# Block fetches spread over slots, deeper buffers and reordered last steps in a one-core attention and mixture-of-experts layer

## Chip, cores and metric

The kernel runs on one core of one Trainium2 chip. The metric is the device time of one execution in microseconds, on the slowest (here the only) core; lower is better. Several runs are taken, and their median is the kernel's time.

## What is computed

The input x has shape (8, 256, 256): eight sequences of 256 tokens, 2048 tokens in all, with 256 features, in float32. Two residual sub-layers follow each other:

```python
x = x + layernorm(attention(layernorm(x)))
x = x + layernorm(experts(layernorm(x)))
```

Attention has 16 query heads and 4 key/value heads of size 128, layer norms on queries and keys, rotary tables and a causal softmax. The second sub-layer, which the change concerns, sends each token to two of eight experts and adds a shared one:

```python
weights, indices = top_k(softmax(xf @ gate_w.T), 2)      # per token, renormalised
h = silu(xf @ w_gate[e]) * (xf @ w_up[e])                # 176 hidden units, e chosen
out = sum over the two e of weight_e * (h @ w_down[e])
out += sigmoid(xf @ shgate_w) * ((silu(xf @ shw_gate) * (xf @ shw_up)) @ shw_down)
```

## The kernel before

**Attention** comes first, sequence by sequence, as a pipeline of small steps written out in a fixed order (lines 325 to 789). For each tile of 128 tokens it ends in the normalised rows, which are written to a table `xf_rows` in DRAM (L606), and in the routing: which two experts, with which weights, at which place of that expert's list (L617 to L702).

**The experts' stage** starts at L1043. All tokens' choices are sorted by expert into NB = 39 blocks of 128 rows, every block for one expert. The tokens are cut into four groups (ENDS = 4, 9, 13, 16 tiles), and the blocks are laid out group after group, so that after block FULL[g] (15, 25, 33, 39) all results for the tiles of group g are there. `table`, `rows_of` and `sources` work out which token stands in which row of which block (`src`); `experts` (L881) works out the addresses `offs` of each block's weights, which TensorE's sequencer loads into registers four blocks at a time (L959).

A loop over slots s = 0 to NB + 2 (L1064) is a software pipeline in a hand-written order. Each engine has one queue and goes through it in this order; it waits only where an instruction needs a semaphore. In slot s stand:

- `fetch` of later blocks (L939): an indirect DMA, issued on GpSimd (POOL), gathers 128 rows from `xf_rows` into a buffer `xb`. There are AHEAD + 1 = 13 buffers; a fetch whose buffer is still to be read waits for that block's transposes on TensorE.
- `turn_block(s)` (L947): two transposes on TensorE into `xt`, a copy `xT` on VectorE.
- `open_block(s - 1)` (L956): four weight-load and matmul passes into `gu`; ScalarE takes the silu into `slb` (L973), VectorE multiplies into `h` (L975).
- `close_block(s - 3)` (L988): matmuls into `py`, a copy `yb` on ScalarE (L998, three buffers), and a DMA of the block's 128 result rows to a table `ys` in DRAM, issued on SP (L999).
- `turn_hidden(s - 2)` (L979): transposes of `h` and a copy on ScalarE (L985).
- one step of the shared expert (`fill(1)`, L1080), while any are left; `fill(n)` takes the next n steps of the list that L297 makes. A step has matmuls (L270 or L286), an activation on ScalarE and, for L270, a product on VectorE (L279). It has nothing on POOL or SP.
- for tiles whose time has come (`when`, L1055 to L1060): `collect` (L1002), two indirect DMAs on POOL that gather a tile's two result rows per token from `ys`; two slots later `combine` (L1013), four VectorE steps, and after each odd tile a power on POOL (L1033) that gives both tiles' reciprocal deviations; then `leave_tile` (L1037), two VectorE steps (L251, L1040) and a DMA of the finished tile on SP (L1041).

The tiles of the last group are collected behind the loop (L1090), which also finishes the shared expert.

The fetches are paced in the program's order by this line; with four fetched ahead of the loop, it lets two stand in each slot until the fetches are 12 blocks ahead, then one:

```python
for b in range(ready, min(ready + 2, s + AHEAD + 1, NB)):
    fetch(b)
    ready = b + 1
```

Of the kernel before, what the change touches and what calls it, by code (L numbers as in the profile page):

```python
# [9 lines left out]
F32 = mybir.dt.float32  # L10
# [9 lines left out]
P = 128  # L20
B, S, HID = 8, 256, 256
# [14 lines left out]
NB = T * TOPK // P + E - 1  # L36
# [6 lines left out]
FULL = [end * TOPK + E - 1 for end in ENDS]  # L43
# [4 lines left out]
def block_kernel(  # L48
# [89 lines left out]
    for j, w in enumerate((wg, wu)):  # L138
# [22 lines left out]
        fill=NEG,  # L161
# [87 lines left out]
    def norm_apply(dst, src, name):  # L249
        mean, rstd = stats.pop(name)  # L250
        nc.vector.tensor_scalar(dst, src, mean, rstd, ALU.subtract, ALU.mult)  # L251
# [67 lines left out]
    def fill(n):  # L319
        for f in todo[:n]:  # L320
            f()
        del todo[:n]


    with ExitStack() as actx:
# [406 lines left out]
        with tc.manual_schedule():  # L732
# [7 lines left out]
            for s in range(B * NS + OUT + 5):  # L740
# [4 lines left out]
                u, j = s - LAG, s  # L745
# [56 lines left out]
    fw = ctx.enter_context(tc.tile_pool(name="fw", bufs=3))  # L802
# [31 lines left out]
    def table():  # L834

        pn = ps_tr.tile([P, NP], F32, tag="tr", name="total")
        nc.tensor.matmul(
            pn, lhsT=ones, rhs=count.rearrange("p g e -> p (g e)"), start=True, stop=True
        )
        n = fc.tile([P, NP], U32, name="n")  # L840
        nc.vector.tensor_scalar(n, pn, P - 1.0, None, ALU.add)
        nc.vector.tensor_scalar(n, n, P.bit_length() - 1, None, ALU.logical_shift_right)
        upto = nb[:, E:]
        nc.vector.tensor_copy(upto, n)

        end = fc.tile([P, NP], F32, name="end")
        nc.vector.tensor_tensor_scan(
            end, upto, nb[:, :NP], 0.0, ALU.add, ALU.subtract
        )

        off = fc.tile([P, NP], F32, name="off")
        nc.vector.tensor_sub(off, upto, end)
        nc.vector.tensor_add(off, off, lift.rearrange("p g e -> p (g e)"))
        nc.vector.tensor_sub(jump[:, : NP - 1], off[:, 1:], off[:, : NP - 1])

        past = fc.tile([P, NP], F32, name="past")
        more = fc.tile([P, 1], F32, name="more")
        nc.vector.scalar_tensor_tensor(
            past, end, part, jump, ALU.is_le, ALU.mult, accum_out=more
        )  # L860
        pickT = fc.tile([P, P], F32, name="pickT")
        nc.vector.tensor_scalar(pickT, aside, more, None, ALU.is_equal)
        load["pickT"], load["upto"], load["off"] = pickT, upto, off

    def rows_of():
        ps = ps_tr.tile([P, NB], F32, tag="tr", name="pickp")
        nc.tensor.transpose(ps, load["pickT"][:NB, :], ident[:NB, :NB])
        pick = fc.tile([P, NB], F32, name="pick")
        nc.vector.tensor_copy(pick, ps)
        load["pick"] = pick  # L870

    def sources():
        ps = ps_tr.tile([P, NB], F32, tag="tr", name="whose")
        nc.tensor.matmul(ps, lhsT=member, rhs=load["pick"], start=True, stop=True)
        src = fc.tile([P, NB], U32, name="src")
        nc.vector.tensor_copy(src, ps)
        load["src"] = src
        load["row"] = ps_tr.tile([1, NB], F32, tag="tr", name="row")
        nc.tensor.matmul(load["row"], lhsT=part, rhs=load["pick"], start=True, stop=True)

    def experts():  # L881

        er = fc.tile([1, NB], I32, name="er")
        nc.vector.tensor_copy(er, load["row"])
        nc.vector.tensor_scalar(er, er, (T // P).bit_length() - 1, None, ALU.logical_shift_right)
        eb = fc.tile([1, NB], F32, name="eb")
        nc.vector.tensor_copy(eb, er)
        nc.vector.tensor_scalar_min(eb, eb, E - 1.0)
        offs = fc.tile([1, 2, NB + LB], I32, name="offs")
        nc.vector.memset(offs, 0)  # L890
        for k, w in enumerate((2 * HE, HID)):
            nc.vector.tensor_scalar_mul(offs[:, k, :NB], eb, float(w))
        load["offs"] = offs
# [40 lines left out]


    state = {}
    AHEAD = 12

    def fetch(b):  # L939
        x_b = fw.tile([P, HID], F32, tag="xb", name=f"xb_{b}", bufs=AHEAD + 1)  # L940
        nc.gpsimd.indirect_dma_start(  # L941
            out=x_b, out_offset=None, in_=xf_rows,
            in_offset=bass.IndirectOffsetOnAxis(ap=load["src"][:, b : b + 1], axis=0),
        )
        state["x", b] = x_b

    def turn_block(b):  # L947
        tr = ps_tr.tile([P, KC, P], F32, tag="tr", name=f"xt_{b}")
        x_b = state.pop(("x", b))
        for c in range(KC):  # L950
            nc.tensor.transpose(tr[:, c, :], x_b[:, c * P : (c + 1) * P], ident)  # L951
        xT = fw.tile([P, KC, P], F32, tag="xT", name=f"xT_{b}")
        nc.vector.tensor_copy(xT, tr)
        state["xT", b] = xT
# [24 lines left out]
    def turn_hidden(b):  # L979
        tr = ps_tr.tile([P, KC, P], F32, tag="tr", name=f"ht_{b}")  # L980
        h = state.pop(("h", b))
        for c in range(KC):
            nc.tensor.transpose(tr[:, c, :], h[:, c * P : (c + 1) * P], ident)  # L983
        hT = fw.tile([P, KC, P], F32, tag="hTb", name=f"hTb_{b}")
        nc.scalar.copy(hT, tr)  # L985
        state["hT", b] = hT

    def close_block(b):  # L988
        hT = state.pop(("hT", b))
        py = ps_sc.tile([P, HID], F32, tag="sc", name=f"py_{b}")  # L990
        off = state.pop(("doff", b))
        for c in range(KC):
            nc.tensor.matmul(  # L993
                py, lhsT=hT[:, c, :], rhs=wd_sb[:, c, bass.ds(off, HID)],
                start=(c == 0), stop=(c == KC - 1),
            )
        y = fw.tile([P, HID], F32, tag="yb", name=f"yb_{b}")
        nc.scalar.copy(y, py)  # L998
        nc.sync.dma_start(out=ys[b * P : (b + 1) * P, :], in_=y)  # L999

# [36 lines left out]
    def leave_tile(i):  # L1037
        y = state.pop(("yo", i))
        norm_apply(y, y, f"d_{i}")
        nc.vector.tensor_add(y, y, x_all[:, i, :])  # L1040
        nc.sync.dma_start(out=out[i * P : (i + 1) * P, :], in_=y)  # L1041

    with tc.manual_schedule():  # L1043
        table()
        fill(2)
        rows_of()
        fill(2)
        sources()
        fill(4)
        ready = 4  # L1050
        for b in range(ready):
            fetch(b)
        experts()

        when = {}  # L1055
        for g, end in enumerate(ENDS):
            begin = ENDS[g - 1] if g else 0
            step = (FULL[g + 1] - FULL[g]) / (end - begin) if g + 1 < G else 0.0
            for i in range(begin, end):
                when[i] = FULL[g] + 3 + int((i - begin) * step)  # L1060
        finding = places()
        late = ENDS[-2]
        LATE = 5
        for s in range(NB + 3):  # L1064
            for b in range(ready, min(ready + 2, s + AHEAD + 1, NB)):
                fetch(b)
                ready = b + 1
            if s < NB:
                turn_block(s)
            if 0 <= s - 1 < NB:  # L1070
                open_block(s - 1)
            if 0 <= s - 3:
                close_block(s - 3)
            if 0 <= s - 2 < NB:
                turn_hidden(s - 2)
            if 2 <= s < G + 3:
                next(finding)

            if s >= 8 and len(todo) > LATE:
                fill(1)  # L1080
            for i in range(late):
                if when[i] == s:
                    collect(i)
            for i in range(late):
                if when[i] == s - 2:
                    combine(i)
                if i % 2 == 1 and when[i] == s - 3:
                    leave_tile(i - 1)
                    leave_tile(i)
        for i in range(late, NTILES):  # L1090
            collect(i)
        fill(LATE)
        for i in range(NTILES):
            if when[i] > NB:
                combine(i)
            if i % 2 == 1 and when[i] > NB - 1:
                leave_tile(i - 1)
                leave_tile(i)
        assert not todo


# [45 lines left out]
```

## Time and profile before

| what | us |
|---|---|
| median of 3 runs | 849.34 |
| lowest and highest run | 846.38, 850.0 |
| the profiled execution | 845.26 |
| its span, first to last instruction | 843.6 |
| mean granted TensorE clock of it | 0.973 of full speed |
| experts' stage: first fetch to the last instruction | 671.1 to 843.6 |

| instructions of the stage | count | mean us of one |
|---|---|---|
| fetch, POOL, L941 | 39 | 0.97 |
| collect, POOL, L1007 | 32 | 0.98 |
| write of block results, SP, L999 | 39 | 128 KB each |
| write of a finished tile, SP, L1041 | 16 | 128 KB each |

The span is what the profile covers, from the first instruction to the last; the profiled execution's own time has 1.66 us more around it. The page gives busy times by engine (PE is TensorE's matmuls, PEld its weight loads, DVE VectorE, ACT ScalarE, POOL GpSimd, SP SyncE); a timeline gives each instruction's start and duration and, in brackets, how long the engine had been idle before it and what ended that. "issue" and "remote" there mean that nothing in the profile, or a signal whose sender it doesn't tell, ended it. Matmuls' ends are modelled, not observed.

### The profile page before, as it was taken

To read this page: it belongs to the slowest core of one execution; us is meant where nothing else is said; L and a number is where in the kernel's file an instruction comes from. 1 tells how busy PE (TensorE), PEld (TensorE's weight loads), DVE (VectorE), ACT (ScalarE), POOL (GpSimd) and SP (SyncE) were. 2 spreads that over 40 slices of the span, in tenths; PEclk is the share of its full clock that TensorE was granted. 3 is DMA by queue.
4 is the path that set the end of the run, shared out by engine and by line. 5 is a ranking of instruction groups with operands and counts; after the bars stand their busy time and mean duration, and the time that the engine had idled before them with its cause. 6 is when DMAs were issued, how large, how long until landed. Compare 5 with 4: busy or idle time off the path is not lost. (4 is left out here: it accounts for less than half of the span.)

```text
span 843.6 us, 11873 instructions
## 1 busy us (share of the span) xinstructions
PE 751.6 (89%) x3770; PEld 552.9 (66%) x3770; DVE 552.8 (66%) x1392; ACT 433.5 (51%) x1393; POOL 486.2 (58%) x523
## 2 busy tenths in 40 slices
PE   4478999999999999999999999998979949998891
PEld 1245667777676677777767777776858827776661
DVE  4586666788778778877877886677644423225675
ACT  1247767656657666675766567565512313333330
POOL 3387587667848757684875768386111162244543
PEclk9789999999999999999999999999999988999997
DMA  8500000000000000000000000004002032224442
GB/s 264 161 1 1 1 1 1 7 1 7 7 1 7 1 7 1 7 7 2 7 1 7 2 7 7 1 7 138 7 13 75 13 94 82 63 88 112 139 126 75
DMA packets 27485, 32.66 MB, mean 39 GB/s; under 512 B 3040, under 2 KB 23616, under 8 KB 27424
## 3 DMA queue, kind: packets, MB, share of 16 engines
q1 hardware_dynamic: 24016, 22.59, 8.5%
q0 software_dynamic: 3408, 9.31, 4.0%
q8 instruction: 31, 0.51, 0.2%
q14 instruction: 30, 0.25, 0.1%
HBM read 22.59 MB, written 9.31 MB: 38 GB/s over the span
## 5 line engine op out<-in xcount | busy, mean ns | idle before, releaser
L366 PE MATMUL qkv<-w_qkv,xnT 128*128 128x512 f32 x384 | 186.6, 610 | 7.3 <-DVE w_qkv L231 3.2
L408 ACT ACTIVATE qn<-qkv,rstds 128x128 f32<-128x128 f32 x320 | 91.2, 368 | 160.7 <-POOL rstds L399 160.7
L399 POOL TENSOR_TENSOR rstds<-ves,nhalf 128x4 f32<-128x4 f32 x80 | 86.9, 1086 | 115.4 <-DVE ves L390 115.4
L434 POOL TENSOR_TENSOR t<-qn,sg_q 128x256 f32<-128x256 f32 x128 | 121.9, 971 | 50.5 <-ACT qn L408 50.5
L581 PE MATMUL o<-wo_sb,oT 128*128 128x256 f32 x512 | 127.2, 387 | 0.0
L482 PE MATMUL sc<-kT,q 128*128 128x128 f32 x768 | 110.1, 278 | 0.9 <-ACT q L471 0.9
L513 ACT ACTIVATE ex<-sc,nmx 128x128 f32<-128x128 f32 (+1 forms) x256 | 107.6, 453 | 2.7 <-DVE nmx L502 2.4
L562 PE MATMUL av<-pT,v 128*128 128x256 f32 (+1 forms) x320 | 101.1, 430 | 7.9 <-ACT oT L573 7.2
L366 PEld LDWEIGHTS qkv<-w_qkv,xnT 128*128 128x128 f32 x384 | 68.1, 197 | 59.9 <-issue 50.4
L482 PEld LDWEIGHTS sc<-kT,q 128*128 128x128 f32 x768 | 102.1, 194 | 4.4 <-ACT q L471 2.4
L581 PEld LDWEIGHTS o<-wo_sb,oT 128*128 128x128 f32 x512 | 91.9, 192 | 9.4
L455 DVE TENSOR_TENSOR t<-t,t 128x512 f32<-128x512 f32 x80 | 55.3, 691 | 51.3 <-POOL t L447 51.3
L470 PEld LDWEIGHTS tq<-ident,t 128*128 128x128 f32 x320 | 38.6, 142 | 69.3 <-issue 50.3
L447 POOL TENSOR_TENSOR t<-t,bb_q 128x512 f32<-128x512 f32 x64 | 81.6, 1275 | 3.0
L549 DVE COPY pT<-tp 128x512 f32<-128x512 f32 x96 | 65.5, 682 | 16.6 <-PE tp L544 16.4
L533 ACT ACTIVATE ex<-ex,rr 128x256 f32<-128x256 f32 x128 | 59.5, 526 | 28.5 <-DVE rr L521 28.5
L562 PEld LDWEIGHTS av<-pT,v 128*128 128x128 f32 x320 | 58.5, 190 | 20.1 <-ACT oT L573 10.4
L941 POOL DMA_INDIRECT xb<-xf_rows,src x39 | 37.7, 966 | 56.6 <-PE xt L951 35.1
L470 PE MATMUL tq<-ident,t 128*128 128x128 f32 x320 | 49.7, 279 | 22.8 <-DVE t L455 22.8
L390 DVE TENSOR_REDUCE ves<-sq 128x4 f32<-128x516 f32 x80 | 54.8, 685 | 21.6 <-ACT sq L384 21.6
L544 PEld LDWEIGHTS tp<-ident,ex 128*128 128x128 f32 x384 | 47.6, 142 | 30.7 <-ACT q L471 10.2
L502 DVE TENSOR_REDUCE nmx<-sc 128x2 f32<-128x512 f32 (+1 forms) x96 | 64.1, 668 | 3.9 <-PE sc L482 3.4
(180 smaller groups left out, 1309.6 us busy)
## 6 DMA issues: line engine op xcount, KB each, us to landing
ys<-yb SPq DMA_DIRECT2D x39, 128.0 KB
w_qkv<-in_wqkvT SPq DMA_DIRECT2D x6, 512.0 KB
x_all<-in_x SPq DMA_DIRECT2D x8, 256.0 KB
wo_sb<-in_woT SPq DMA_DIRECT2D x1, 2048.0 KB
xf_rows<-xf SPq DMA_DIRECT2D x16, 128.0 KB
out<-yo SPq DMA_DIRECT2D x16, 128.0 KB
wgu_sb<-in_wg SPq DMA_DIRECT2D x2, 704.0 KB
wgu_sb<-in_wu SPq DMA_DIRECT2D x2, 704.0 KB
```

The source lines that it names most:

```text
L366: nc.tensor.matmul(ps.rearrange("p h d -> p (h d)"), lhsT=seqs[b]["xnT"][t][:, c, :], rhs=w_qkv[g][:, c, :], start=(c == 0), stop=(c == KC ...
L399: nc.gpsimd.tensor_tensor(rstd, now.pop(("ve", b, j)), nhalf, ALU.pow)
L408: nc.scalar.activation(qn[:, h, :], ps[:, h, :], AF.Copy, scale=rstd[:, h : h + 1])
L434: nc.gpsimd.tensor_tensor(t2[:, :, lo : lo + HD], qn[:, :, hi : hi + HD], sg[s][:, t : t + 1, lo : lo + HD].to_broadcast([P, REP, HD]), AL ...
L447: nc.gpsimd.tensor_tensor(t2, t2, bb[s][:, t : t + 1, :].to_broadcast([P, REP, D]), ALU.add)
L470: nc.tensor.transpose(tr[:, h, :], t1[:, h, :], ident)
L482: nc.tensor.matmul(sc[:, h, k * P : (k + 1) * P], lhsT=seqs[b]["qT"][g][:, r0 + h, t * P : (t + 1) * P], rhs=seqs[b]["kT"][:, g, k * P : ( ...
L502: nc.vector.tensor_reduce(out=nm, in_=now["sc", b, u], axis=AX.X, op=ALU.max, negate=True)
L513: nc.scalar.activation(ex[:, h, :], sc[:, h, :], AF.Exp, bias=nm[:, h : h + 1], accum_out=rs[:, h : h + 1],)
L549: nc.vector.tensor_copy(pT, now.pop(("tp", b, u)).rearrange("p c q -> p (c q)"))
L562: nc.tensor.matmul(now["av"][:, r0 : r0 + nh, :].rearrange("p h q -> p (h q)"), lhsT=seqs[b]["v"][:, k, g * D : (g + 1) * D], rhs=pT[:, k ...
L581: nc.tensor.matmul(now["o", b, t], lhsT=seqs[b]["oT"][h // REP, t][:, h % REP, :], rhs=wo_sb[:, h, :], start=(h == 0), stop=(h == H - 1),)
```

## The change

Five edits, all in the experts' stage:

1. AHEAD goes from 12 to 14, so that there are 15 buffers for fetched rows.
2. The fetches stand one in even slots and two in odd ones until slot FULL[0] + 2 = 17, and then one in each odd slot. The bound by the lead over s goes. As before, four stand ahead of the loop, and fetches 0 to 30 stand ahead of the first collect.
3. `yb` has six buffers, not the pool's three.
4. `experts` comes ahead of the four steps of the shared expert that stood before it; the first four fetches do so too.
5. Of a pair of tiles, the even one's `leave_tile` stays in its slot, and the odd one's goes one slot later. Behind the loop, tiles that have not left by then leave in pairs as before.

```diff
-    AHEAD = 12
+    AHEAD = 14
...
-        y = fw.tile([P, HID], F32, tag="yb", name=f"yb_{b}")
+        y = fw.tile([P, HID], F32, tag="yb", name=f"yb_{b}", bufs=6)
...
         sources()
-        fill(4)
         ready = 4
         for b in range(ready):
             fetch(b)
         experts()
+        fill(4)
...
         for s in range(NB + 3):
-            for b in range(ready, min(ready + 2, s + AHEAD + 1, NB)):
+            n = 1 + s % 2 if s < FULL[0] + 3 else s % 2
+            for b in range(ready, min(ready + n, NB)):
                 fetch(b)
                 ready = b + 1
...
-                if i % 2 == 1 and when[i] == s - 3:
-                    leave_tile(i - 1)
+                if when[i | 1] == s - 3 - i % 2:
                     leave_tile(i)
...
-            if i % 2 == 1 and when[i] > NB - 1:
-                leave_tile(i - 1)
-                leave_tile(i)
+            for j in (i - 1, i) if i % 2 else ():
+                if ("yo", j) in state:
+                    leave_tile(j)
```

## The prediction

> **What bounds the kernel now.** I read the page first, then the windows of the mixture-of-experts stage, then its timeline engine by engine, since the diff touches nothing before 663 us. TensorE (PE) is the bound of the whole: 89% of the span.
>
> ```profile
> span 843.6 us, 11873 instructions
> PE 751.6 (89%) x3770; PEld 552.9 (66%) x3770; DVE 552.8 (66%) x1392; ACT 433.5 (51%) x1393; POOL 486.2 (58%) x523
> ```
>
> The windows below cut the stage up (columns: stretch, length, busy time of PE, PEld, DVE, ACT and POOL, granted clock, DMA share, GB/s). From 702 to 748 PE has no gap. It loses about 9.7 us of 14 in the second line, then runs at half clock for the third; 748 to 814 loses 3.3 and 2.9 us.
>
> ```profile
> 682.00:696.00 14.00, 4.34 (x18) 2.40 (x17) 2.89 (x9) 1.49 (x6) 8.47 (x10) 0.85 0.30 91
> 696.00:702.00 6.00, 6.00 (x15) 4.35 (x16) 2.36 (x7) 1.15 (x4) 1.45 (x2) 0.51 0.27 87
> 702.00:748.00 46.00, 46.00 (x222) 36.26 (x221) 13.05 (x36) 15.92 (x47) 11.47 (x12) 1.00 0.23 70
> 748.00:782.00 34.00, 30.68 (x146) 23.20 (x145) 14.99 (x42) 10.90 (x34) 16.24 (x17) 1.00 0.38 108
> 782.00:814.00 32.00, 29.06 (x135) 21.36 (x134) 22.04 (x62) 10.86 (x35) 15.88 (x17) 1.00 0.43 128
> ```
>
> The timeline of the lost 9.7 us (start, duration, engine, instruction, idle time before it and what ended it):
>
> ```profile
> 681.50 0.38 PE L983 MATMUL ht<-ident,h 128*128 128x128 f32 x2
> 681.94 1.35 PE L968 MATMUL gu<-wgu_sb,xT 128*128 x4
> 683.90 0.37 ACT L985 COPY hTb<-ht 128x256 f32<-128x256 f32 x1 [1.88 <-PE gu L968]
> ...
> 691.50 0.96 POOL L941 DMA_INDIRECT xb<-xf_rows,src  x1 [0.30 <-issue]
> 693.07 0.32 ACT L973 ACTIVATE slb<-gu 128x176 f32<-128x176 f32 x1 [8.80 <-remote]
> 695.54 0.95 POOL L941 DMA_INDIRECT xb<-xf_rows,src  x1 [3.09 <-remote]
> 695.92 2.08 PE L993 MATMUL py<-wd_sb,hTb 128*128 x4 [7.08 <-ACT hTb L985]
> ```
>
> PE shows gu of block 2 done at 683.29, but ScalarE, with nothing else to do, starts on it at 693.07. Nothing is wanting but the news that PE is done: it is 2.0 us late for block 0's ht, 4.6 for block 3's xt, 9.8 here. All this time POOL issues row fetches back to back, 17 of them, one each 1.26 us, from 671.09 to 692.45; the news comes 0.6 us after the last. I looked for the same elsewhere. It is late by 1.6 to 2.6 us at the end of the POOL runs of 6 (to 756.87), 8 (to 778.30) and 6 (to 792.73), never in the runs of 4. **So a long unbroken run of indirect DMAs on POOL is what costs PE time here**, by the trace; why, it doesn't say. After 814 the end is POOL's as well: six last collects, two powers and the last tiles.
>
> ```profile
> PE 2%; POOL 1%; issue 1%; DVE 1%; POOLq 0%; ACT 0%; DVEq 0%
> ```
>
> **What the Trainium skill says.** "Perfetto Trace Analysis", the section on a Tensor Engine instruction: the end shown is estimated, and the signal goes out only when PSUM has acknowledged the write. The trace agrees so far that an end need not be the moment of the news (9.8 us apart). "DMA: Bandwidth & Descriptors", Anatomy of one DMA, SWDGE path: about 2.0 us fixed plus bytes/436e3, so an estimate of 2.3 us for 128 KB; in the trace the fetch begun at 688.97 lands at 691.7, 2.7 us. "TensorE: Matmul & The Clock Gate", Part 1: an idle window halves the clock; the 0.51 above agrees. No page that I found says that a run of POOL DMAs holds up PE's signals.
>
> **The change, part by part.** I sum against the profiled execution, 845.26 us (span 843.6 and 1.66 around it), 4.08 below the median of the runs, 849.34; the differences go on the median.
>
> **Fetches, first run.** The new pace is only an order in POOL's queue, and ahead of the first collect that queue holds fetches 0 to 30 and nothing else, before and after. So the pace holds nothing back; what stops POOL is the buffers. With 13, fetch 13 needs xt of block 0, and fetch 17 needs xt of block 4, whose news is late: the run is 17. With 15, fetch 15 needs block 0 and fetch 19 needs block 4: the run is **19**. Two more at 1.26 are 2.5 us: its end goes from 692.45 to about 694.97, the gu news from 693.07 to 695.6, PE's restart from 695.92 to 698.4. +2.5; the ends are 0 (the news isn't tied to the last fetch) and +5 (see the rivals). The half clock, which now lasts until 701.94 in the clock record, may end there again, with 2.5 us less work in it (-1.3), or a 3.4 us step later (+0.5): I take 0.
>
> **Fetches from step 18 on.** They no longer come in pairs, but stand between collects. What ends a run on POOL is a power that waits for a combine, or a collect that waits for blocks. Between those, the queue read in order gives runs of 6, 1, 1, 8, 6, 4 before and 6, 7, 8, 5 after (the eight after step 28 are tiles 4 to 6 with fetches 36 and 37). PE's idle time at these places before: 0.3, then about 2.1 (1.71, and 1.31 less the 0.93 that the same address step, with a run of 4, has at 808), then 1.04, then none. Priced by length: before 3.4, after 0.3 + 1.5 + 2.1 + 0.3 = 4.2. **+0.8**, ends -0.6 and +2.5. Waits queued behind: the power of tiles 4 and 5 comes two fetches later, 2.5 us, and L251 waits for it on VectorE, with the next xT behind; but only one tile leaves in that slot, which saves 0.9 there, and VectorE has some 10 us idle of 32. 0.3 at most, within the ends. Fetch 38 stands late in the queue, near 799, for a block turned near 810: enough.
>
> **Addresses sooner.** VectorE makes offs at 676.2 to 676.7, and PE's sequencer waits 0.80 us for it at L959. Moved ahead of two L279 products it is done near 671.7, in an idle time of 1.71 us, and the products don't slip; the four steps of fill have no instruction on POOL or SP, and stand as before in PE's and ScalarE's queues. PE starts gu of block 0 0.8 us sooner, once its address loads (0.5 and 1.0 us) are through. But next late is the held news: 0.8 us more to wait before 693.07. I take 0; the ends are -0.8, and -2.5 if one more slot gets through before the hold begins.
>
> **Six buffers for yb.** ScalarE's copy waited for PE 26 times (17.1 us) and never for its DMA: 0. If the write were slow, three buffers still cover three slots, 7.5 us, against a landing of 2 to 3.
>
> **Last steps in two slots.** Moves two VectorE steps of 0.42 and one 0.34 us DMA issue on SP per pair by one slot, and ys of the next block goes ahead of it on SP. No collect waits on those ys rows last: the last ys goes at 819.52, its collects wait on POOL for the power at 821.97. 0. Without VectorE's idle time it would be worth 0.9 us a pair, either way.
>
> Sum: +2.5 + 0.8 + 0 + 0 + 0 = +3.3: 848.6 for the profiled execution, **852.6** on the median, with its own range of 849.5 to 855. That is within 0.5% (4.2 us), about what a measurement of this kernel can tell from no change.
>
> **Rivals.**
> *The longer run feeds itself (slower, 22%).* The news that leaks out at 683.9 and 686.7 frees buffers. If that of block 4's xt (done 687.66) comes before 695.3, fetches 19 and 20 join without a break: two more, +2.5, and the clock +0.5, and later runs at their upper end +1.7: 849.34 + 3.3 + 4.7, about 857. For it: each fetch that needed xt 0 to 3 found it. Against it: in the kernel before block 4's news was 8 us late.
> *The start gets ahead of the hold (faster, 22%).* The news is prompt until 681.7 and late from 681.9 on. Ended 0.8 us sooner, ht of block 0 and xt of block 3 are out before that; if the hold then begins with the next signals at 2.0 and 4.6 us rather than 9.8, one to two slots of 2.5 us are saved: -5 to -6, about 844. Against it: gu of block 2 still ends inside, at 682.5.
> *It does nothing (14%).* The pace doesn't pace, and the hold ends when it will: 0 to -0.8, about 849.
> The forecast itself has 42%, 6 of it above 0.5%.
>
> **How the numbers follow.** Faster by over 0.5%: 22% and a little of the third, 0.23. Slower: 22 + 6, 0.28. Between: 0.49. The range for 8 in 10 runs from 843, which takes in the middle of the faster rival, to 857, the middle of the slower.
>
> **What would show it.** POOL's first run: 19 fetches to about 695 (right), 17 or fewer, or gaps in it (wrong: the pace does pace). PE's restart on py of block 1 near 698.4. Runs 6, 7, 8, 5 later, with PE idle near the ends of the 7 and the 8. gu of block 0 near 678.0 instead of 678.84. ScalarE's yb waits as before; the stretch after PE's last block as long as before. If PE loses as much with a longer run as before, run length isn't the cause, and the sum falls.

## The result and the profile after

| | us |
|---|---|
| before, median of 12 runs (lowest, highest) | 847.78 (846.06, 850.1) |
| after, median of 12 runs (lowest, highest) | 850.25 (848.48, 853.68) |
| ratio after to before, 95% interval | 1.0033 [1.0017, 1.0048] |
| profiled execution, before and after | 845.26 and 850.27 |

By the ratio the change costs 2.8 us (1.4 to 4.1 by the interval); the medians lie 2.5 us apart. The ratios in this document are those on record. They lie near the quotient of the means and not that of the medians, so a difference by ratio and one by medians can be up to 2 us apart; the text says which is meant where it matters. The change is slower by less than the 0.5% that the forecast called "within". The profiled executions lie 5.0 us apart, more than the medians: the one of before is faster than all twelve runs above.

The page of the changed kernel, its span and first part:

```profile
span 848.6 us, 11838 instructions
PE 750.1 (88%) x3739; PEld 551.7 (65%) x3770; DVE 552.2 (65%) x1392; ACT 433.8 (51%) x1393; POOL 486.6 (57%) x523
```

The busy times are those of before within 1.5 us. Nothing was added to any engine's work; what is new is waiting. The same windows as before tell where (columns: stretch, length, busy time of PE, PEld, DVE, ACT and POOL, granted clock, DMA share, GB/s):

```profile
682.00:696.00 14.00, 4.72 (x15) 2.27 (x14) 2.16 (x8) 0.69 (x2) 10.07 (x11) 0.72 0.36 107
696.00:702.00 6.00, 2.94 (x9) 2.46 (x10) 1.98 (x6) 1.61 (x5) 0.95 (x1) 0.50 0.18 57
702.00:748.00 46.00, 46.00 (x212) 35.73 (x212) 13.19 (x37) 15.37 (x45) 10.52 (x11) 0.97 0.23 69
748.00:782.00 34.00, 32.35 (x152) 24.34 (x150) 13.96 (x41) 10.97 (x34) 13.42 (x14) 1.00 0.31 93
782.00:814.00 32.00, 27.34 (x124) 19.68 (x125) 20.84 (x61) 10.29 (x33) 16.47 (x18) 1.00 0.43 125
```

The second line is the change: from 696 to 702 PE now stands for 3.06 us, where before it was busy throughout. From 748 on, 1.65 us are lost where 3.3 were, and then 4.66 where 2.9 were: less than 0.1 more in sum.

Chosen lines of the timeline of the same place (start, duration, engine, instruction, idle time before it and what ended that):

```profile
681.52 1.35 PE L968 MATMUL gu<-wgu_sb,xT 128*128 x4
682.78 0.37 ACT L985 COPY hTb<-ht 128x256 f32<-128x256 f32 x1 [1.17 <-issue]
...
694.16 0.96 POOL L941 DMA_INDIRECT xb<-xf_rows,src  x1 [0.30 <-remote]
694.09 0.32 ACT L973 ACTIVATE slb<-gu 128x176 f32<-128x176 f32 x1 [10.94 <-remote]
698.68 0.95 POOL L941 DMA_INDIRECT xb<-xf_rows,src  x1 [3.56 <-remote]
699.06 1.22 PE L993 MATMUL py<-wd_sb,hTb 128*128 x2 [9.03 <-ACT hTb L985]
```

The fetch at 694.16 is the nineteenth without a break; the first stood at 671.25. ScalarE waits 10.94 us for a `gu` that PE shows finished at 682.87, and PE's restart moves from 695.92 to 699.06.

### The profile page after: what moved, and what is told of

Its sections match the earlier page's. It is cut to its first block, busy times and chain, and to the rows that moved or that the text cites. A ratio compares the mean times of both kernels' runs of the same rounds, so it can differ in the third digit from the quotient of the medians.

```text
span 848.6 us, 11838 instructions
## 1 busy us (share of the span) xinstructions
PE 750.1 (88%) x3739; PEld 551.7 (65%) x3770; DVE 552.2 (65%) x1392; ACT 433.8 (51%) x1393; POOL 486.6 (57%) x523
## 4 chain that ended last, share of the span: by engine, by line
PE 54%; POOL 17%; DVE 13%; ACT 8%; issue 5%; another core or an unknown queue 2%; DMA 0%; POOLq 0%; ACTq 0%; DVEq 0%
PE qkv L366 11%; PE o L581 7%; PE sc L482 6%; POOL rstds L399 6%; ACT qn L408 5%; POOL t L434 5%; PE av L562 5%; PE gu L968 5%; PE py L993 4%; POOL t L447 3%; PE tp L544 3%; PE tq L470 2%; PE g L270 2%; PE u L270 2%; PE sd L286 2%
```

## The experiments

Theory: the length of POOL's first unbroken run of row fetches sets how long PE's news is held, and two more buffers made it two fetches longer. Rivals: another of the edits costs the time; the transfers, not their issuing, hold the news, by their traffic or by a growing number of fetches under way; the hold has nothing to do with the run, or is there only while the profiler records.

Two numbers of each trace are used throughout: the delay of `gu` of block 2 (from its end as PE shows it to the start of ScalarE's silu), and the **start stretch** (from the first fetch to the turning of block 5 on PE). The second doesn't depend on how long attention took in that execution, which differed by 2.7 us between traces.

### Which edit

One part of the change taken back, on the changed kernel:

```diff
-        x_b = fw.tile([P, HID], F32, tag="xb", name=f"xb_{b}", bufs=AHEAD + 1)
+        x_b = fw.tile([P, HID], F32, tag="xb", name=f"xb_{b}", bufs=13)
...
-            for b in range(ready, min(ready + n, NB)):
+            for b in range(ready, min(ready + n, s + 13, NB)):
```

> The changed kernel with 13 buffers for fetched rows again, and with the lead bounded at 13 blocks as such buffers need; everything else of the change stays. If the number of buffers sets the length of GpSimd's first unbroken run of row fetches, and the run's length the time for which TensorE's signals are held back: 17 fetches instead of 19, the first fetch run ending near 692.5, TensorE's restart on py of block 1 near 696, and 2.5 to 3 us less than the changed kernel, so within 1 us of the kernel before. If another part of the change (order of later fetches, addresses, last steps, six result buffers) makes the difference: the time stays about 3 us above the kernel before.

Measured: 846.88, ratio to the kernel before 0.9999 [0.9987, 1.001]; first run 17. Its windows:

```profile
682.00:696.00 14.00, 6.52 (x23) 3.45 (x22) 3.12 (x10) 1.01 (x3) 9.56 (x10) 0.77 0.35 104
696.00:702.00 6.00, 4.11 (x11) 3.15 (x12) 2.37 (x6) 1.61 (x5) 1.87 (x2) 0.50 0.21 66
```

This execution began its fetches 1.9 us later than that of before, so its lines can't be laid on those directly: its run ends at 694.31, and the start stretch is 27.2 us, as before (27.1), against 30.1 after. With 13 buffers the whole loss is gone.

The opposite, on the kernel before: `bufs=AHEAD + 1` made `bufs=15`, and nothing else.

> The kernel before with one edit: 15 buffers for fetched rows instead of 13 (its lead stays at 12). Run-length theory: the first run has 19 fetches (or 17, if the lead in the program's order should pace it after all), and the time is 2.5 to 3.1 us above the kernel before. If the order of the fetches or another part of the change makes the difference: no change, within 0.5 us.

Measured: 852.67 against 846.5, ratio 1.0064 [1.0044, 1.0084]: 5.4 us by the ratio, 6.2 by the medians, more than expected. The first run has 19 fetches and the start stretch is 30.0, so that part is as expected; the rest arises later. Chosen lines of PE's timeline there:

```profile
765.90 0.44 PE L951 MATMUL xt<-ident,xb 128*128 128x128 f32 x2 [1.32 <-DVE xT L953]
767.74 2.71 PE L968 MATMUL gu<-wgu_sb,xT 128*128 x4 [1.40 <-issue]
781.09 1.45 PE L968 MATMUL gu<-wgu_sb,xT 128*128 x4 [1.50 <-issue]
789.21 1.13 PE L993 MATMUL py<-wd_sb,hTb 128*128 x4 [1.70 <-ACT hTb L985]
```

The runs of later fetches and collects, 6, 1, 1, 8, 6 in the kernel before, are 8, 8, 6 here: with more buffers POOL no longer pauses between them. The first of the new runs of 8 (753.87 to 763.65) is followed by the first two lines, and by half clock (the `gu` passes of 767.74 take 2.71 us, those of 781.09 take 1.45). So the edit of the order, with its runs of 6, 7, 8, 5, wins about 2.6 us back once there are 15 buffers (5.4 less 2.8, by the ratios). This is a difference between two comparisons, uncertain by about 2 us to either side, and it includes the three other edits, which by themselves are worth nothing that shows (below). With 13 buffers the order did nothing that shows.

The other three edits on the kernel before (six result buffers, addresses sooner, last steps in two slots), then the addresses alone, the other two alone, and all three once more:

> The kernel before with the three edits that the forecast put at nothing, and no other: six result buffers, addresses made sooner, last steps in two slots. Forecast: within 0.5 us of the kernel before (the addresses at most -0.8, swallowed by the held news). If an earlier start gets ahead of the hold: 2.5 to 5 us below.

> The kernel before with one edit: experts and the first four fetches ahead of the four steps of the shared expert. The three edits without the fetches measured 2.4 us below the kernel before (0.4 to 3.7 by its interval), where the forecast had 0. If the addresses are what was mis-sized: all of it here, 2 to 2.5 us below, with gu of block 0 about 0.4 us sooner after the first fetch and less lost before 702. If they are worth nothing: within 0.8 us of the kernel before.

> The kernel before with the other two edits: six result buffers and the last steps of a pair in two slots. If these are what was mis-sized: 2 to 2.5 us below the kernel before, with less idle time on TensorE between 748 and 814. If they are worth nothing: within 0.8 us.

> The three edits without the fetches once more. Together they measured 2.4 us below the kernel before; the addresses alone, and the other two alone, both measured nothing (within 1.5 us). If the gain is real and needs both: again about 0.997 of the kernel before. If it was the kernel before that stood high among its own runs on that chip (848.85, against 846.5 and 847.8 elsewhere): within 0.15% of it here.

| edits on the kernel before | median | before on the same chip | ratio, 95% |
|---|---|---|---|
| all three | 846.52 | 848.85 | 0.9972 [0.9957, 0.9987] |
| addresses | 848.2 | 847.83 | 1.0009 [0.9995, 1.0024] |
| other two | 845.53 | 847.83 | 0.9996 [0.9974, 1.0018] |
| all three again | 847.99 | 847.12 | 1.0003 [0.9985, 1.0022] |

The first line looks like a gain of 2.4 us. The repeat doesn't have it. The start stretch is 27.2 to 27.3 us in all four. The medians of the kernel before lie between 846.5 and 848.85 in the four sets of runs of these experiments, as far apart as that gain. The three edits are worth nothing that these runs can show.

### Whether the run is the cause

A shorter run, by fewer buffers, on the kernel before:

```diff
-    AHEAD = 12
+    AHEAD = 4
```

> The kernel before with a lead of 4 blocks and 5 buffers, so that each fetch waits for a block that TensorE has just turned and the first run has at most about 9 fetches. Run-length theory: the news is held for at most 2 to 3 us, TensorE's idle time of about 9.7 us before 696 falls to 3 or less, the half clock after it goes too, and the time is 8 to 12 us below the kernel before. If the hold has nothing to do with the run, or is there only while the profiler records: the timed runs stay within 1 us of the kernel before, or are slower where a fetch comes too late for its block (a fetch takes 2.7 us to land, a slot 2.5).

Measured: 844.65 against 846.5, ratio 0.9971 [0.996, 0.9983], so 2.5 us by the ratio (1.9 by the medians), not 8 to 12. The windows tell why:

```profile
682.00:696.00 14.00, 13.73 (x66) 10.12 (x65) 9.01 (x26) 4.86 (x16) 5.75 (x6) 1.00 0.30 95
696.00:702.00 6.00, 6.00 (x31) 4.64 (x30) 1.83 (x5) 2.22 (x7) 1.30 (x2) 1.00 0.28 89
702.00:748.00 46.00, 46.00 (x219) 36.31 (x219) 10.41 (x30) 15.50 (x45) 14.26 (x16) 1.00 0.25 75
748.00:782.00 34.00, 29.10 (x136) 21.43 (x135) 18.85 (x53) 10.85 (x33) 18.19 (x19) 1.00 0.39 117
782.00:814.00 32.00, 24.13 (x107) 17.74 (x105) 18.65 (x52) 8.78 (x27) 18.09 (x21) 0.95 0.43 124
```

The first two lines are what the theory asked for: a first run of 7, no idle PE, full clock, a start stretch of 16.1 us, 11.0 less. The last two give most of it back. With a lead of 4 the later fetches stand between the collects, POOL's runs there grow to 9 and 10, and PE stands for 4.9 and 7.9 us where it stood for 3.3 and 2.9. The signal of `gu` of block 2, and one of those later waits:

```profile
684.05 1.35 PE L968 MATMUL gu<-wgu_sb,xT 128*128 x4
685.43 0.32 ACT L973 ACTIVATE slb<-gu 128x176 f32<-128x176 f32 x1 [1.03 <-PE gu L968]
790.00 2.08 PE L993 MATMUL py<-wd_sb,hTb 128*128 x4 [5.48 <-ACT hTb L985]
```

A lead between the two, AHEAD = 8:

> The kernel before with a lead of 8 blocks and 9 buffers, between the 5 and 13 tried. Run-length theory: the first run has 9 + 3 or 4, so 12 or 13 fetches, and TensorE's news is held for about 5 us; that stretch gains about 5 us on the kernel before, where 5 buffers gained about 10; the later fetches, behind collects in the queue as with a lead of 4, give some 2 to 4 of it back. 1 to 4 us below the kernel before. If the hold is on or off and not in proportion: the first stretch as with 13 buffers or as with 5.

Measured: 845.13 against 848.85, ratio 0.9954 [0.994, 0.9969]. The first run is 12, the start stretch 22.3 (4.8 less than before), and in its trace 4.6 us are given back later, behind runs of 9 and 8.

Then the same number of bytes by plain DMAs from SyncE. This version leaves out the gather: it fetches 128 consecutive rows, not the chosen ones.

```diff
-        nc.gpsimd.indirect_dma_start(
-            out=x_b, out_offset=None, in_=xf_rows,
-            in_offset=bass.IndirectOffsetOnAxis(ap=load["src"][:, b : b + 1], axis=0),
-        )
+        r = b % NTILES * P
+        nc.sync.dma_start(out=x_b, in_=xf_rows[r : r + P, :])
```

> The kernel before with every row fetch made a plain DMA of 128 consecutive rows issued on SyncE, with the same bytes, buffers and lead; the gather by token is left out, so the rows are not the chosen ones. It tells GpSimd's issuing from the transfers. If GpSimd's unbroken run of indirect DMAs holds the signals: no hold before the first collect, and 8 to 13 us below the kernel before. If the 2 MB of fetched rows hold them (traffic): the hold stays, and the time is within 3 us of the kernel before.

Measured: 832.11 against 846.5, ratio 0.983 [0.9812, 0.9848]. The windows:

```profile
682.00:696.00 14.00, 13.77 (x68) 10.39 (x67) 8.77 (x27) 5.34 (x17) 0.00 (x0) 1.00 0.37 114
696.00:702.00 6.00, 6.00 (x30) 4.51 (x29) 1.67 (x5) 1.73 (x6) 0.00 (x0) 1.00 0.30 89
```

From 682 to 696 the transfers move 114 GB/s, more than the 91 of the kernel before, and PE stands for 0.23 us. So traffic at this rate doesn't hold the news. The comparison isn't clean in two respects: plain fetches need no `src`, so the first 12 went ahead of 671; and in the trace their packets have 1 KB each, on another queue, where those of the gather have 4 KB. It tells the amount of traffic from the cause, not the kind of transfer.

### The pace enforced

The changed order paces nothing unless POOL really waits. A small POOL instruction makes it do so (line numbers of the lines below it go up by four):

```diff
+    def beat(b):
+        mark = small.tile([P, 1], F32, tag="mark", name=f"mark_{b}")
+        nc.gpsimd.tensor_tensor(mark, state["xT", b][:, 0, 0:1], nhalf[:, 0:1], ALU.mult)
...
+            if 1 <= s < FULL[0] + 3:
+                beat(s - 1)
             for b in range(ready, min(ready + n, NB)):
```

> The changed kernel with its pace enforced: in slots 1 to 17 a one-column multiplication on GpSimd, which reads the transposed rows of the block before, stands ahead of the slot's fetches, so that GpSimd waits once per slot; 15 buffers, order and everything else stay. Run-length theory: the first run is 5 to 7 fetches, then 1 or 2 at a time; the hold of 11.2 us and TensorE's idle time behind it go, and so does the half clock to 705; the lead of one block more than needed suffices for a landing of 2.7 us. 10 to 13 us below the changed kernel, so 7 to 11 below the kernel before. If the transfers or the number of buffers held the signals: within 2 us of the changed kernel. If waiting on GpSimd delays fetches so that blocks come late: slower than the changed kernel.

Measured: 837.78 against 848.85, ratio 0.9868 [0.9842, 0.9894], with all 15 buffers. Chosen lines of POOL's timeline:

```profile
683.14 0.20 POOL L949 TENSOR_TENSOR mark<-xT,nhalf 128x1 f32<-128x1 f32 x1
683.49 0.98 POOL L941 DMA_INDIRECT xb<-xf_rows,src  x1 [0.15 <-issue]
684.78 0.95 POOL L941 DMA_INDIRECT xb<-xf_rows,src  x1 [0.30 <-issue]
686.46 0.19 POOL L949 TENSOR_TENSOR mark<-xT,nhalf 128x1 f32<-128x1 f32 x1 [0.73 <-issue]
686.79 0.98 POOL L941 DMA_INDIRECT xb<-xf_rows,src  x1
691.10 0.19 POOL L949 TENSOR_TENSOR mark<-xT,nhalf 128x1 f32<-128x1 f32 x1 [3.32 <-DVE xT L957]
```

The first run was expected at 5 to 7 and is 10: until 684 POOL is behind, finds each beat's block turned, and the beat doesn't stop it. Standing between fetches for 0.2 us does not break the run; the news of `gu` of block 2 comes at 688.74, 4.3 us late, after POOL has really paused. So the start stretch falls to 18.2 us and not to 16.

More buffers, and nearly all fetches ahead of the first collect:

```diff
-    AHEAD = 14
+    AHEAD = 22
...
-            n = 1 + s % 2 if s < FULL[0] + 3 else s % 2
+            n = 1 + s % 2 if s < 8 else 2
```

> The same, with 23 buffers and two fetches in each slot from slot 8 on, so that all but the last two or three fetches stand ahead of the first collect. Run-length theory: the first hold is gone as in the version with 15 buffers, 23 buffers lengthen no run since the pace doesn't rest on them, and the runs of 7 and 8 between collects shrink to 4 and 6: another 1 to 3 us below that version. If buffers as such cost: above it by 2 us or more. Two fetches in a slot of 3.8 us could also join into one run (two take 2.5 us): then a hold shows between 715 and 750.

Measured: 834.4 against 848.85, ratio 0.9819 [0.9792, 0.9845]: by the medians 3.4 us below the version with 15 buffers (five runs of each, which don't overlap). Its first run is 11, its start stretch 18.2 again with 23 buffers. The runs of 7 and 8 between the collects are gone (4 and 6 in their place), and PE stands for 1.0 us between 748 and 782, against 2.4 in the version with 15 buffers.

Last, a slower start, so that POOL waits from the first slots on:

```diff
-            n = 1 + s % 2 if s < 8 else 2
+            n = 1 if s < 4 else 1 + s % 2 if s < 8 else 2 + s % 2
```

> The version with 23 buffers and the kept pace, with a slower start: one fetch in slots 0 to 3, then one and two, and from slot 8 on two and three in turn, so that GpSimd really waits once per slot from the first, and all fetches stand ahead of the first collect. In the version before it, the first run still had 11 fetches and the news was 4.6 us late. Run-length theory: a first run of 7 or less, no late news before 702, no half clock there, and 3 to 6 us less than that version, about 829 to 831. If the hold comes from the number of fetches under way and not from their following each other without a pause: no gain.

Measured: 830.1 against 847.83, ratio 0.9803 [0.9778, 0.9828], the fastest version that does the whole work: by the medians 17.7 us below the kernel before (16.7 by the ratio) and 20 below the changed one. Its windows, and chosen lines of POOL's timeline and of the signal of `gu`:

```profile
682.00:696.00 14.00, 13.44 (x64) 10.02 (x64) 8.83 (x26) 5.21 (x17) 8.83 (x14) 1.00 0.37 111
696.00:702.00 6.00, 6.00 (x31) 4.59 (x30) 0.34 (x1) 1.44 (x4) 3.81 (x5) 1.00 0.54 154
702.00:748.00 46.00, 45.19 (x215) 35.62 (x214) 12.25 (x34) 15.88 (x47) 24.59 (x32) 1.00 0.41 101
748.00:782.00 34.00, 32.25 (x153) 24.11 (x152) 21.30 (x61) 12.24 (x38) 13.90 (x15) 1.00 0.34 106
```

```profile
681.44 0.19 POOL L949 TENSOR_TENSOR mark<-xT,nhalf 128x1 f32<-128x1 f32 x1 [0.30 <-issue]
681.78 0.99 POOL L941 DMA_INDIRECT xb<-xf_rows,src  x1
684.26 0.19 POOL L949 TENSOR_TENSOR mark<-xT,nhalf 128x1 f32<-128x1 f32 x1 [1.49 <-DVE xT L957]
684.59 1.03 POOL L941 DMA_INDIRECT xb<-xf_rows,src  x1
681.93 1.35 PE L972 MATMUL gu<-wgu_sb,xT 128*128 x4
683.74 0.32 ACT L977 ACTIVATE slb<-gu 128x176 f32<-128x176 f32 x1 [1.13 <-PE py L997]
```

POOL has as much to do from 682 to 696 as before (8.83 us busy against 8.47), and the DMAs move more bytes (111 GB/s against 91). What differs is that POOL waits 1.49 us at 684.26, after a run of 8, and PE's news of `gu` is 0.5 us late instead of 9.8. The run of 8 is one longer than expected, and the news of block 3's `xt` was still 1.7 us late behind it.

All traces with fetches on POOL side by side. From 10 fetches to 17 and 19 the delay grows with the first run, whatever made the run long or short:

| first run | kernels | delay of gu of block 2, us | start stretch, us |
|---|---|---|---|
| 7 | lead 4 | 0.0 | 16.1 |
| 8 | slow start | 0.5 | 14.6 |
| 10, 11 | pace enforced, all fetched | 4.3, 4.6 | 18.2, 18.2 |
| 12 | lead 8 | 4.6 | 22.3 |
| 17 | before, and five others | 8.6 to 11.3 | 27.1 to 27.3 |
| 19 | after, 15 buffers alone | 11.2, 11.9 | 30.1, 30.0 |

Neighbours aren't resolved: 10, 11 and 12 lie together, and the range of 17 meets that of 19. The first two rows need care. There the run was over (at 681.50 and at 682.77) before PE had finished this `gu` (at 685.40 and at 683.28); they show that the signal is prompt outside a run, not that a short run holds nothing.

The timed runs follow the traces (2 to 3 us for 17 to 19, 17.7 for the slow start), so the hold isn't an accident of the traced executions. Each timed run on record has a span and a granted clock too, so these runs don't show whether the hold would be there with no recording at all.

## Why the prediction was right

It named what costs the time, a longer first run of fetches on POOL, and the experiments bear that out. The sum came out near (+3.3 against 2.8 by the ratio) partly because two misses point opposite ways: the first run was put about 0.4 us too low, and the 0.8 for the later fetches doesn't show. Its text counts the lines of its windows one too far: the 9.7 us are lost in the first line shown, and the half clock stands in the second. Its terms one by one:

- **First run, +2.5: right, a little small.** 19 fetches, to 695.11 (forecast 694.97). The start stretch grew by 3.0 us, and the timed price of the two buffers, from the changed kernel with 13 and with 15, is 2.9 us (0.34% of 847.78). The two steps inside were each off: the news came at 694.09, 1.5 sooner than forecast, and PE's restart at 699.06, 0.7 later. The restart hangs on another signal, that of `ht` of block 1, which ScalarE took up at 695.49 before and at 698.63 after. "The news comes 0.6 us after the last" fetch was one execution's number: in the traces with 17 and 19 it came between 1.4 us before and 2.2 after the end of the run.
- **Half clock, 0: right in effect.** From the restart to the turning of block 6 it took 6.6 us before and after. The record showed half clock for 17.07 us (688.1 to 705.2) and not 10.24, because it set in a step sooner, when PE had only one `gu` pass left (2.23 us against 1.35) and then stood idle anyway. The Trainium skill, "TensorE: Matmul & The Clock Gate", Part 1, says that PE idle for a window falls back to half rate; the traces agree: both versions with a first run of 7 or 8 kept 1.00 from 682 to 702, and all with 17 or 19 had 0.50 to 0.87 there.
- **Later fetches, +0.8: the runs were 6, 7, 8, 5 as read from the queue.** PE stood 1.56 us near the end of the 7 (forecast 1.5) and 2.90 near that of the 8 (forecast 2.1). The sum over the gaps is not separated from scatter: the windows of the two traces give less than +0.1, and the changed kernel with 13 buffers, which has these runs, measured -0.1 us (-1.1 to +0.8) against the kernel before, three free edits included.
- **Addresses, six buffers, last steps, 0: right.** `gu` of block 0 started at 678.42, 0.42 sooner and not 0.8 (0.58 sooner, counted from the first fetch): PE's idle time ahead of it fell only from 2.28 to 1.69 us. That the held news took it back, as forecast, fits the start stretch of the kernel with only this edit (27.2 against 27.1). Alone, the addresses measured 1.0009, the other two 0.9996.
- **Stretch after PE's last block: longer by 1.2 us in this trace**, since the last collects came later. The changed kernel with 13 buffers and both runs of the three other edits alone had it as before, within 0.1, and the kernel with only the addresses moved had it longer by 2.2; so it is most likely scatter and no price of the change.

Of the 2.4 us between 852.6 and 850.25, 1.6 are the base (849.34 from three runs, 847.78 from twelve) and 0.8 the change itself (+3.3 forecast, 2.5 between the medians).

Of the rivals, the run that feeds itself (about 857) didn't occur: the news of block 4's `xt` came at 698.45, 3.3 us after the run had ended. The start that gets ahead of the hold (about 844) failed too: 0.42 us sooner did not save a slot. The third, that it does nothing, lies outside the interval of the ratio, which begins at 1.0017.

One thing stays open. The runs show that POOL's unbroken indirect DMAs cause the delay, that it ends near the end of the run and that as many bytes by plain transfers don't cause it. That POOL's pause ends it is shown less strictly: in three of the eight traces with 17 or 19 fetches the news of `gu` came 0.7 to 1.4 us before the last fetch had ended, though the news behind it waited for the pause. The runs don't show which path the fetches and PE's signals share. The Trainium skill, "Perfetto Trace Analysis", on a DMA instruction issued by GpSimd, says that its end in the profile is the end of writing its descriptors, not of the transfer; the traces agree (0.96 us busy in the kernel before, and 2.7 us from its start until its semaphore was last raised), but whether the writing or what is still under way holds the signal wasn't separated.

Three more things in the traces narrow it. First, they record when each semaphore was raised. PE's in the kernel before stand at 683.87, 686.72 and 693.04, and then five within 0.2 us, from 695.16 to 695.34, 2.7 us after the last fetch of the run; after the change four come from 698.34 to 698.48. So the raising itself is late, not the engine that waits for it, and what was held comes out together. Second, ScalarE's and VectorE's signals to PE were not late in the same run: a copy on ScalarE ended at 684.27 and PE went on at 684.32, one on VectorE at 687.16 and PE at 687.22. Third, no backlog of fetches grows: by the recorded packets, each fetch of that run ended 2.3 to 3.3 us after its start, the seventeenth (2.4) no later than the second (2.4).

## What to carry to other kernels

An order in a queue is no pace: where POOL's queue held nothing else, it ran through it as fast as the buffers allowed, and more buffers meant a longer burst (5, 9, 13 and 15 buffers gave first runs of 7, 12, 17 and 19). Before deepening a buffer ask what makes the producer pause, and whether anyone gains from that pause. Here making POOL wait for a consumer (0.2 us of work a slot) was worth 11 us, and 17 to 18 with more buffers and an order that goes with it, while two more buffers alone cost 5 to 6.

## What had not been expected of the hardware

- The delay of one and the same PE signal grew with POOL's first run: 4.3 to 4.6 us at 10 to 12 fetches, about 9 to 11 at 17 (21.4 us), 11 to 12 at 19 (23.9 us). Early in a run signals were still prompt: in the kernel before, `gu` of block 1 was done at 681.67, 10.6 us into the run, and taken up at 681.70.
- Only PE's signals were seen to be late, and they were let out in a burst; those of ScalarE and VectorE came through in the same run within 0.1 us.
- A 0.2 us POOL instruction without a wait between two indirect DMAs doesn't break a run; within a pause of 1.5 us, behind a run of 8, the held signals came.
- With 5 buffers the run between the collects, 10 indirect DMAs from 774.45 to 787.11, made PE wait 5.48 us in one place: it isn't a matter of the first fetches alone.
- The kernel before has a median between 846.5 and 848.85 from one set of runs to another, so that one comparison with a nominal interval of 0.15% to each side showed a gain of 0.28% that a repeat didn't show.
